# Sixteen-head attention on one core: the extra pieces of a step move into the bank of the burst of values

## The chip, the core and the metric

The kernel runs on one NeuronCore of a Trainium2 chip. Five engines run their own instruction queues: TensorE (PE in the profile; its weight loads are PEld), VectorE (DVE), ScalarE (ACT), GpSimd (POOL) and SyncE (SP, which here only starts transfers). The metric is device time of one execution in microseconds (us). Before the change the median of three runs is 1695.35 us (1690.04 to 1696.96). The profile comes from one further execution.

## What is computed

The input x is 8 sequences of 512 tokens with 128 features. Four layers follow each other, each with a residual and a layer norm. The change concerns the first and third, two attentions with 16 heads of 8 features:

```python
qkv = x @ W_qkv.T + b_qkv                        # 128 -> 3 * 128
scores = einsum('bhqd,bhkd->bhqk', q, k) / sqrt(8)
probs = softmax(scores + bias)                   # layer 0 only: bias = -slope[h] * |i - j|
out = einsum('bhqk,bhkd->bhqd', probs, v)
x = layernorm(x + out @ W_out.T + b_out)
```

The second layer is a gated feed-forward with operands rounded to a 4-bit grid in blocks of 16; the fourth is two blocks of windowed attention and a gated feed-forward. The change does not touch these two.

## The kernel before

Both attentions run through one function, `attention(li, ...)` (L250), with li 0 or 1. The work is cut into units: one sequence b and one group g of four heads, 32 units in all. `q` and `k` of a sequence lie transposed in SBUF as eight pairs of heads, one head in partitions 0 to 63 and one in 64 to 127, in two buffers that sequences take in turn. A unit is 8 half-steps of scores and, 16 half-steps later (`LAG`), 8 half-steps of weights. The main loop (L467) takes two half-steps at a time; this text calls one turn of it a step, and places are counted in half-steps, so a unit is 4 steps and a sequence 16 steps (places 0, 2, ... 30).

In each step PE gets, for t = 0 and 1:

- `scores`: two matmuls of 512 columns into a tile `s_ps` of two PSUM banks (pool `as`, two such tiles). DVE reduces it to the row maxima `m`.
- `weights`: the transposed product of another unit, two matmuls into two banks `t_ps`, in layer 0 with small corrections for the bias (`corrected`). ACT takes the exponential of each into `e` (four per step, 512 columns each).

Then come the extras, which a dictionary `todo`, filled by `later(place, function, ...)` in `plan` (L403), holds for each place:

- `values` (L338), one in each step: a burst of 16 matmuls that multiply a unit's exponentials with the values of its heads, into 128 columns of a bank `av`. The values carry a column of ones, so the sums of the softmax come out beside the products. ACT copies `av` into `avs`.
- `shift` (L324), one step in four: one transposition of `m` into `m_ps`, an ACT copy `mt`, two small DMAs started by POOL, which put the negative maxima into the last row of `q`.
- a piece, in 12 of 16 steps: `divide` (a unit's four transposes into `o_ps`, a reciprocal and a multiply on DVE), `begin_x`, `begin_qk` and `begin_v` (transpose and projections of the next sequence: `xt_ps`, `qk_ps`, `v_ps`, each taken out by ACT), `end_o` and `end_y` (transpose and output projection of the finished sequence: `ot_ps`, taken out by ACT, and `y_ps`, added to `xs` by DVE). `measured` takes the statistics of the result.

`begin_qk` further splits its result into two parts on POOL (a cast and a subtraction), SP writes them to DRAM (`far`), and `load_qk` reads them back in the layout of `q` or `k` with eight DMAs per quarter.

The PSUM tiles of pool `at` have two names, t0 and t1, with two banks each. Step z calls `weights` with rings z % 2 and then (z + 1) % 2, so each call takes both banks of one name. The extras of step z take banks of name z % 2: the burst one, the piece the other, a shift likewise. In the next step that name is used by the second `weights`.

PE runs in program order, `Kept` and `tc.keep_in_program_order` hold the written order on all engines, and the tile framework adds the waits. The loop also chooses the order inside a step: where the step before held a piece (`pieces`, L466), `weights` stands ahead of `scores`, otherwise behind:

```python
for f, a in sorted(todo.pop(z), key=lambda x: first.index(x[0]) if x[0] in first else len(first)):
    f(*a)        # first = [values, shift]; then the pieces
```

In the profile all matmuls of the attentions have line L256 and all transposes L257 (the helpers `mm` and `tr`), what goes through `Kept` has L48, SP's writes of `far` L225 and its reads L237. So instructions are told apart by their tiles.

Of the kernel before, what the change touches and what calls it, by code (L numbers as in the profile page):

```python
# [9 lines left out]
F32 = mybir.dt.float32  # L10
# [4 lines left out]
ALU = mybir.AluOpType  # L15
# [3 lines left out]
P = 128  # L19
B, S, D = 8, 512, 128  # L20
# [31 lines left out]
def body(ctx, tc, x, consts, rows, wa0, wa1, acols, bo, wf, wqkv, wo, w1, w2, cols, b2r, qs, ks, out):  # L52
# [136 lines left out]
    def in_tiles(mm, dst, lhsT, rhs):  # L189

        for r in range(0, P, 32):
            mm(dst[r : r + 32], lhsT=lhsT[:, r : r + 32], rhs=rhs, start=True, stop=True)

    def operand_steps(li, qs_, ks_, va, mm, tr, bank, work, dram, qb):
        w, col = wa[li], acol[:, li]

        def begin_x(b, h):
            ps = bank("xt_ps")
            for c in range(NT):
                tr(ps[:, c * P : (c + 1) * P], xn[:, b * NT + c, :], ident)  # L200
            h["xT"] = work.tile([P, S], F32, tag="xT", name="xT", bufs=1)
            act_.copy(h["xT"], ps)

        def begin_qk(b, h, n, start=nc.sync.dma_start, part=None):

            at = slice(0, S) if part is None else slice(part * S // 2, (part + 1) * S // 2)
            ps = bank("qk_ps")[:, at]
            in_tiles(mm, ps, w[:, n * P : (n + 1) * P], h["xT"][:, at])
            if part != 1:
                h["x"] = work.tile([P, S], F32, tag="x", name="x", bufs=1)  # L210
            t = h["x"]
            if n == 0:
                act_.activation(t[:, at], ps, AF.Identity, bias=qb, scale=col[:, 0:1])
            else:
                act_.activation(t[:, at], ps, AF.Identity, bias=col[:, 2:3])
            if part == 0:
                return
            parts = work.tile([P, 2, S], F32R, tag=f"hl{n}", name="parts", bufs=1)
            hi, lo = parts[:, 0, :], parts[:, 1, :]
            pool_.tensor_copy(hi, t)  # L220
            pool_.tensor_tensor(lo, t, hi.bitcast(F32), ALU.subtract)

            far = dram.tile([2, 2, 64, S], F32R, tag=f"far{n}", name="far")
            for j in range(2):
                start(  # L225
                    out=far[j].bitcast(F32).rearrange("a c t -> c a t"), in_=parts[64 * j : 64 * j + 64].bitcast(F32)
                )
            h["far", n] = far

        def load_qk(b, h, n, part, start=nc.sync.dma_start):  # L230

# [9 lines left out]
        def begin_v(b, h):  # L241
            ps = bank("v_ps").rearrange("p (c d) -> p c d", c=NT)
            for c in range(NT):
                in_tiles(mm, ps[:, c, :], h["xT"][:, c * P : (c + 1) * P], w[:, W_V : W_V + P])
            act_.copy(va[b % 2][:, :, :, 0:8], ps.rearrange("p c (h d) -> p c h d", d=8))

        return begin_x, begin_qk, load_qk, begin_v


    def attention(li, alibi, qs_, ks_, va, batch, late=None, spare=None, alone=0):  # L250
# [7 lines left out]
        with ExitStack() as st:  # L258
# [3 lines left out]
            def bank(name, n=None):  # L262
# [2 lines left out]
                    n = turn[0]  # L265
                return p_t.tile([P, S], F32, tag=f"t{n}", name=name)

            begun = len(batch)
            batch += [{} for _ in range(B - begun)]
            work = crow = None  # L270

            def hold_o(h):
                h["o"] = work.tile([P, NT, P], F32, tag="o", name="o", bufs=3)

            def with_bias(b):
                for c in range(NT):
# [46 lines left out]

            def shift(u):  # L324

                ps = bank("m_ps")[0:16, 0:P]
                tr(ps, u["m"].rearrange("p j a c -> p (j a c)"), ident)
                mt = small.tile([16, P], F32R, tag="mt", name="mt")
                act_.copy(mt, ps)
# [8 lines left out]
            def values(u, pp, c):  # L338

                if pp == 0 and c == 0:  # L340
                    u["avs"] = work.tile([P, NT, P], F32, tag="avs", name="avs")
                av = bank("av")[:, 0:P]
                for blk in range(NT):
                    for j in range(2):
                        for f in range(2):
# [6 lines left out]
                act_.copy(u["avs"][:, 2 * pp + c, :], av)  # L352

            def divide(u):

                ps = bank("o_ps")
                to = ps.rearrange("p (f c a j d) -> p f c a j d", f=2, c=2, a=2, j=2)
                for i in range(NT):
                    tr(to[:, :, i % 2, i // 2], u["avs"][:, i, :], ident)
                ps = ps.rearrange("p (n r c) -> p n r c", n=NT, r=4)  # L360
                den = work.tile([P, NT, 4], F32, tag="den", name="den")
                dve.reciprocal(den, ps[:, :, :, 8])
                g = u["g"]
                dve.tensor_tensor(
                    u["h"]["o"][:, :, g * 32 : (g + 1) * 32].rearrange("p c (r d) -> p c r d", d=8),
                    ps[:, :, :, 0:8],
                    den.unsqueeze(3).broadcast_to([P, NT, 4, 8]),
                    ALU.mult,
                )
                u["e"] = u["avs"] = None  # L370

            def end_o(h):
                ps = bank("ot_ps")
                for c in range(NT):
                    tr(ps[:, c * P : (c + 1) * P], h["o"][:, c, :], ident)
                h["oT"] = work.tile([P, S], F32, tag="oT", name="oT", bufs=1)
                act_.copy(h["oT"], ps)

            def end_y(b, h):
                ps = bank("y_ps").rearrange("p (c d) -> p c d", c=NT)  # L380
                for c in range(NT):
                    in_tiles(mm, ps[:, c, :], h["oT"][:, c * P : (c + 1) * P], w[:, W_O : W_O + P])
                i0, h["bn"] = b * NT, small.tile([P, NT, 6], F32, tag="bn", name="bn")
                dve.tensor_tensor(xs[:, i0 : i0 + NT, :], ps, xs[:, i0 : i0 + NT, :], ALU.add)

            def measured(b, h, lo, hi):
                for c in range(lo, hi):
# [15 lines left out]
            def plan():  # L403
# [1 line left out]
                const, work = pool("ac", 1), pool("aw", 2)  # L405
                dram = pool("ad", 2, space=bass.MemoryType.DRAM)
                begin_x, begin_qk, load_qk, begin_v = operand_steps(
                    li, qs_, ks_, va, mm, tr, bank, work, dram, qb[:, li : li + 1]
                )

                bvb = const.tile([P, P], F32, name="bvb")
# [3 lines left out]
                for n in range(B * G):  # L415
# [3 lines left out]
                    for i in range(NT):  # L419
                        later(z + 4 + 2 * i, values, units[n], *divmod(i, 2))  # L420
                    if g == 0 and begun <= b + 1 < B:
                        nxt = (b + 1, batch[b + 1])
                        order = (0, 6, 8, 14, 16) if b else (8, 10, 12, 14, 16)
                        for at, f in zip(order, (begin_x, *[begin_qk] * 4)):
                            i = order.index(at) - 1
                            later(s + at, f, *nxt, *((i // 2, nc.sync.dma_start, i % 2) if i >= 0 else ()))
                        for at, n_, part in ((14, 0, 0), (18, 0, 1), (22, 1, 0), (26, 1, 1)):
                            later(s + at, load_qk, *nxt, n_, part)
                        later(s + 22, begin_v, *nxt)
                        later(s + 22, with_bias, b + 1)  # L430
                    if g == 0:
                        later(s + 20 if b else alone, hold_o, batch[b])
                    if g == G - 1:
                        if b < B - 1:
                            times = (z + 16, z + 22, z + 24, z + 26)
                        else:
                            times = (z + 14, z + 16, z + 16, z + 16)
                        later(times[0], end_o, batch[b])
                        later(times[1], end_y, b, batch[b])
                        later(times[2], measured, b, batch[b], 0, 2)  # L440
                        later(times[3], measured, b, batch[b], 2, NT)
# [17 lines left out]
                if late:  # L459
                    late()  # L460
                if spare:
                    spare(later, lambda b: (b * G + G - 1) * NU + LAG + 32, work, bank, mm, tr, p_s)
                turn[1] = 0

            first, loaded = [values, shift], False
# [1 line left out]
            for z in range((B * G * NU + LAG + 20) // 2):  # L467
# [1 line left out]
                    plan()  # L469
                n, i = divmod(2 * z, NU)  # L470
                m, k = divmod(2 * z - LAG, NU)
                turn[0] = z % 2
                heavy, loaded = loaded, any(f.__name__ in pieces for f, _ in todo.get(z, []))
                for t in range(2):
                    if 0 <= m < B * G and heavy:
# [699 lines left out]
    with tc.tile_pool(name="ops", bufs=1) as ops:  # L1175
# [27 lines left out]
        def first_spare(later, done, work, bank, mm, tr, p_s):  # L1203
# [3 lines left out]
                quantize_weights(later, 28 + 11 * j, j, temps, work, bank, tr)  # L1207

            def tokens(b):
                for i, f in zip((0, 4, 6, 8), quantized_tokens(b, *temps(), work)):  # L1210
                    later(done(b) + i, f)

            for b in range(B - 1):
# [14 lines left out]
            h, end = {}, done(B - 1) - 32 + 4 * NT  # L1228
# [66 lines left out]
def _attention_layout(w_qkv, b_qkv, w_out):  # L1295
# [6 lines left out]
    w[:, W_O : W_O + P] = w_out.T  # L1302
    c = np.zeros((P, 4), np.float32)
    c[:, 1], c[:, 2], c[:, 3] = b_qkv[0:P][order], b_qkv[P : 2 * P][order], b_qkv[2 * P :]
    return w, c, order // 8


# [40 lines left out]
```

## Time and profile before

| | |
|---|---|
| profiled execution, its own time | 1685.9 us |
| its span, first to last instruction | 1684.1 us |
| granted TensorE clock, mean | 0.969 |
| busy: PE, DVE, ACT, POOL | 1563.3, 1372.5, 1264.0, 915.5 us |
| bursts of values of layer 0, first to last of 126 | 63.9 to 464.8 us |
| bursts of values of layer 1, first to last of 126 | 604.8 to 976.3 us |
| two more bursts per layer follow another without a pause and are counted with it | |

Between the two lie the rest of layer 0 and the feed-forward; after 980 us the fourth layer runs, 42% of the span. A line of the timeline gives start, duration, engine, source line, operation, output tile, input tiles, shapes, and in brackets how long the engine was idle before it and what ended that. The duration of a merged line (x4) covers all of its instructions. A burst's line shows x32, since each fp32 matmul is issued as two.

### The profile page before, as it was taken

To read this page: it belongs to the slowest core of one execution; us is meant where nothing else is said; L and a number is where in the kernel's file an instruction comes from. 1 tells how busy PE (TensorE), PEld (TensorE's weight loads), DVE (VectorE), ACT (ScalarE), POOL (GpSimd) and SP (SyncE) were. 2 spreads that over 40 slices of the span, in tenths; PEclk is the share of its full clock that TensorE was granted. 3 is DMA by queue.
4 is the path that set the end of the run, shared out by engine and by line. 5 is a ranking of instruction groups with operands and counts; after the bars stand their busy time and mean duration, and the time that the engine had idled before them with its cause. 6 is when DMAs were issued, how large, how long until landed. Compare 5 with 4: busy or idle time off the path is not lost.

```text
span 1684.1 us, 50766 instructions
## 1 busy us (share of the span) xinstructions
PE 1563.3 (93%) x20544; PEld 1056.3 (63%) x20545; DVE 1372.5 (81%) x2220; ACT 1264.0 (75%) x3214; POOL 915.5 (54%) x974
## 2 busy tenths in 40 slices
PE   2989999999988899999999879999999999999995
PEld 1556766666655656666666556666666666666664
DVE  3878888898578998888889668888888888888863
ACT  0577888888745578888888767788888888888873
POOL 3222323332247722333322469888888888888882
PEclk7899999999998889999999999999999999999998
DMA  6733233222010432332222121111111111111110
GB/s 123 150 76 98 53 78 78 59 49 57 11 13 1 76 78 78 78 78 62 60 61 69 30 53 33 39 36 36 37 38 36 36 36 36 42 42 42 36 36 25
DMA packets 92843, 90.79 MB, mean 54 GB/s; under 512 B 45969, under 2 KB 58257, under 8 KB 92610
## 3 DMA queue, kind: packets, MB, share of 16 engines
q1 hardware_dynamic: 87280, 85.49, 23.0%
q8 instruction: 163, 2.67, 0.7%
q10 hardware_dynamic: 1234, 1.52, 0.4%
q0 software_dynamic: 4096, 0.54, 0.2%
q14 instruction: 70, 0.57, 0.1%
HBM read 41.82 MB, written 18.87 MB: 36 GB/s over the span
## 4 chain that ended last, share of the span: by engine, by line
PE 70%; DVE 14%; ACT 5%; POOL 5%; DMA 3%; issue 2%; SPq 0%; ACTq 0%; DVEq 0%; POOLq 0%
PE av L256 13%; PE t_ps L256 10%; PE s_ps L256 7%; DVE m L48 6%; PE y_ps L671 6%; PE sp L671 5%; PE o_ps L671 3%; PE t_ps L671 3%; PE v_ps L671 3%; PE q_ps L671 3%; PE k_ps L671 3%; PE p_ps L671 3%; PE gp L671 2%; ACT e L48 2%; PE ap L671 2%
## 5 line engine op out<-in xcount | busy, mean ns | idle before, releaser
L48 DVE TENSOR_REDUCE m<-s_ps 128x2 f32<-128x1024 f32 x512 | 600.0, 1219 | 90.6 <-PE s_ps L256 84.7
L48 ACT ACTIVATE e<-t_ps 128x512 f32<-128x512 f32 x1024 | 530.2, 603 | 103.0 <-PE t_ps L256 101.9
L256 PE MATMUL s_ps<-k,q 63*128 63x512 f32 x1024 | 281.2, 477 | 40.3 <-DVE m L48 19.4
L256 PE MATMUL av<-e,va 128*32 128x128 f32 x8192 | 279.4, 278 | 14.2 <-ACT e L48 9.0
L256 PE MATMUL t_ps<-q,k 64*128 64x512 f32 x1024 | 270.3, 450 | 2.5 <-DMA q<-mt 0.9
L256 PEld LDWEIGHTS av<-e,va 128*32 128x32 f32 x8192 | 210.9, 110 | 87.3 <-ACT e L48 73.0
L48 POOL DMA_DIRECT2D q<-mt x128 | 68.9, 542 | 348.0 <-ACT mt L48 347.8
L671 ACT ACTIVATE pw<-sp,m,was_v 128x128 f32<-128x128 f32 x512 | 227.5, 479 | 1.6 <-DVE m L671 0.9
L671 POOL TENSOR_TENSOR was_v<-was_v 128x16 f32<-128x16 f32 x64 | 187.8, 2934 | 5.3
L256 PEld LDWEIGHTS t_ps<-q,k 64*128 64x128 f32 x1024 | 133.4, 187 | 85.1 <-ACT avs L48 34.0
L256 PEld LDWEIGHTS s_ps<-k,q 63*128 63x128 f32 x1024 | 120.9, 192 | 76.7 <-DVE m L48 41.6
L671 POOL TENSOR_TENSOR pw<-pw,den 128x1024 f32<-128x1024 f32 x64 | 121.3, 1895 | 7.6 <-DVE den L671 7.6
L671 ACT ACTIVATION_READ_ACCUMULATOR pw<-sp,m,was_v 128x1 f32 x512 | 115.2, 225 | 0.0
L48 POOL CAST parts<-x 128x512 fp32r<-128x512 f32 x32 | 21.7, 678 | 163.9 <-ACT x L48 163.9
L671 DVE TENSOR_REDUCE m<-sp 128x4 f32<-128x512 f32 x128 | 82.3, 684 | 19.0 <-PE sp L671 17.2
L671 ACT COPY v<-v_ps 128x512 f32<-128x512 f32 x64 | 37.7, 590 | 71.6 <-PE v_ps L671 71.6
L671 POOL TENSOR_TENSOR was_k<-was_k,was_q 128x512 f32<-128x512 f32 x64 | 88.1, 1377 | 0.9 <-DVE was_q L671 0.9
L671 PEld LDWEIGHTS t_ps<-cst,was_k 128*128 128x128 f32 x512 | 59.2, 142 | 44.4 <-issue 22.1
L671 DVE COPY pT<-p_ps 128x512 f32<-128x512 f32 x128 | 79.9, 665 | 0.5 <-PE p_ps L671 0.5
L671 PEld LDWEIGHTS p_ps<-cst,pw 128*128 128x128 f32 x512 | 59.8, 141 | 32.3 <-issue 28.0
L48 ACT COPY avs<-av 128x128 f32<-128x128 f32 x256 | 71.1, 278 | 11.6 <-PE av L256 8.7
L671 DVE TENSOR_REDUCE was_v<-was_k 128x16 f32<-128x1024 f32 x64 | 77.1, 1205 | 0.0
(191 smaller groups left out, 3252.8 us busy)
## 6 DMA issues: line engine op xcount, KB each, us to landing
far<-parts SPq DMA_DIRECT2D x64, 256.0 KB
q<-far SPq DMA_DIRECT2D x256, 64.0 KB
k<-far SPq DMA_DIRECT2D x240, 64.0 KB
ve<-v SPq DMA_DIRECT2D x112, 128.0 KB
xn<-in_x SPq DMA_DIRECT2D x8, 256.0 KB
q<-mt POOLq DMA_DIRECT2D x128, 4.0 KB, 3.2
hn<-xs SPq DMA_DIRECT2D x16, 128.0 KB
hn<-xs SPq DMA_DIRECT2D x16, 112.0 KB
```

Source lines behind the costliest of these rows:

```text
L48: return lambda *a, **k: self.tc.keep_in_program_order(f(*a, **k))
L256: mm = lambda *a, **k: tc.keep_in_program_order(nc.tensor.matmul(*a, **k))
L671: kept = lambda f: lambda *a, **k: tc.keep_in_program_order(f(*a, **k))
```

## The change

- A new helper `share(name, lo, n)` gives columns of one bank per step. The burst of values takes columns 0 to 128, a shift columns 128 to 256, a piece columns 256 to 512. If columns are taken already, a new bank is begun; at each step the bank is forgotten.
- All pieces are cut to 256 columns: transposes, values, the output transposes and the output projection of a sequence come as two halves (`part` 0 and 1) at two places; q's and k's projections were halves already. They take one bank's columns 256 to 512 each.
- `divide` writes its four transposes at 9-column distances, each over the unused tail of the one before, in four blocks of 60 columns (240 in all), and multiplies in two halves. The order of features in `o` changes; the rows of the output weights and of the value bias are permuted alike on the host.
- Places within a sequence's 16 steps change: `begin_x` from 0 to 6 and 8; q from 6, 8 to 10, 14; k from 14, 16 to 16, 18; `begin_v` from 22 to 26 and 30; `load_qk` from 14, 18, 22, 26 to 16, 18, 22, 24; `end_o` from 24 to 22 and 24; `end_y` from 30 to 0 and 2 of the next sequence; statistics and the quantization of layer 0's tokens follow. Now each of the 16 steps holds a piece, and the four with a shift hold both.

```diff
+            shared = {"at": None}
+            def share(name, lo=S // 2, n=S // 2):
+                if shared["at"] is None or any(lo < b and a < lo + n for a, b in shared["used"]):
+                    shared["at"], shared["used"] = bank(name), []
+                shared["used"].append((lo, lo + n))
+                return shared["at"][:, lo : lo + n]
...
+        def piece(name, part):
+            if part is None:
+                return bank(name), slice(0, S), range(NT)
+            ps = share(name) if share else bank(name)[:, 0 : S // 2]
+            return ps, slice(part * S // 2, (part + 1) * S // 2), range(2 * part, 2 * part + 2)
...
-        def begin_x(b, h):
-            ps = bank("xt_ps")
-            for c in range(NT):
-                tr(ps[:, c * P : (c + 1) * P], xn[:, b * NT + c, :], ident)
-            h["xT"] = work.tile([P, S], F32, tag="xT", name="xT", bufs=1)
-            act_.copy(h["xT"], ps)
+        def begin_x(b, h, part=None):
+            ps, at, chunks = piece("xt_ps", part)
+            for i, c in enumerate(chunks):
+                tr(ps[:, i * P : (i + 1) * P], xn[:, b * NT + c, :], ident)
+            if part != 1:
+                h["xT"] = work.tile([P, S], F32, tag="xT", name="xT", bufs=1)
+            act_.copy(h["xT"][:, at], ps)
...
-                ps = bank("m_ps")[0:16, 0:P]
+                ps = share("m_ps", P, P)[0:16]
...
-                av = bank("av")[:, 0:P]
+                av = share("av", 0, P)
...
-                ps = bank("o_ps")
-                to = ps.rearrange("p (f c a j d) -> p f c a j d", f=2, c=2, a=2, j=2)
+                ps = share("o_ps")[:, 0:240].rearrange("p (r k) -> p r k", r=4)
                 for i in range(NT):
-                    tr(to[:, :, i % 2, i // 2], u["avs"][:, i, :], ident)
+                    tr(ps[:, :, 9 * i : 9 * i + 32], u["avs"][:, i, :], ident)
+                ps = ps[:, :, 0:36].rearrange("p r (i d) -> p r i d", d=9)
...
+                for f in range(2):
+                    both = slice(2 * f, 2 * f + 2)
+                    dve.tensor_tensor(
+                        u["h"]["o"][:, 4 * f : 4 * f + 4, at : at + 16].rearrange("p i (j d) -> p i j d", d=8),
+                        ps[:, both, :, 0:8].rearrange("p j i d -> p i j d"),
+                        den[:, both, :].rearrange("p j i -> p i j").unsqueeze(3).broadcast_to([P, NT, 2, 8]),
+                        ALU.mult,
+                    )
...
+                        for part in range(2):
+                            later(s + (6 if b else 8) + 2 * part, begin_x, *nxt, part)
+                            later(s + (10, 14)[part], begin_qk, *nxt, 0, sp, part)
+                            later(s + (16, 18)[part], begin_qk, *nxt, 1, sp, part)
+                            later(s + (26, 30)[part], begin_v, *nxt, part)
...
+                        times = (14, 16, 24, 26, 26, 30) if b < B - 1 else (14, 14, 16, 16, 16, 16)
+                        for i, f in enumerate((end_o, end_o, end_y, end_y, measured, measured)):
...
-                turn[0] = z % 2
+                turn[0], shared["at"] = z % 2, None
```

More of the change, by code (lines that the diff above doesn't have):

```diff
@@ L192, in in_tiles, with operand_steps @@
             mm(dst[r : r + 32], lhsT=lhsT[:, r : r + 32], rhs=rhs, start=True, stop=True)
-    def operand_steps(li, qs_, ks_, va, mm, tr, bank, work, dram, qb):
+    def operand_steps(li, qs_, ks_, va, mm, tr, bank, work, dram, qb, share=None):
         w, col = wa[li], acol[:, li]
-        def begin_x(b, h):
-            ps = bank("xt_ps")
-            for c in range(NT):
-                tr(ps[:, c * P : (c + 1) * P], xn[:, b * NT + c, :], ident)
-            h["xT"] = work.tile([P, S], F32, tag="xT", name="xT", bufs=1)
-            act_.copy(h["xT"], ps)
+        def piece(name, part):
[10 more added lines that the diff above has]
+            act_.copy(h["xT"][:, at], ps)
         def begin_qk(b, h, n, start=nc.sync.dma_start, part=None):
-            at = slice(0, S) if part is None else slice(part * S // 2, (part + 1) * S // 2)
-            ps = bank("qk_ps")[:, at]
+            ps, at, _ = piece("qk_ps", part)
             in_tiles(mm, ps, w[:, n * P : (n + 1) * P], h["xT"][:, at])
@@ L239, in load_qk, with begin_v @@
                     )
[L241 to L245, printed above, removed]
+        def begin_v(b, h, part=None):
+            ps, _, chunks = piece("v_ps", part)
+            ps = ps.rearrange("p (c d) -> p c d", d=P)
+            for i, c in enumerate(chunks):
+                in_tiles(mm, ps[:, i, :], h["xT"][:, c * P : (c + 1) * P], w[:, W_V : W_V + P])
+            act_.copy(va[b % 2][:, chunks[0] : chunks[-1] + 1, :, 0:8], ps.rearrange("p c (h d) -> p c h d", d=8))
         return begin_x, begin_qk, load_qk, begin_v
@@ L272, in hold_o @@
             def hold_o(h):
-                h["o"] = work.tile([P, NT, P], F32, tag="o", name="o", bufs=3)
+                h["o"] = work.tile([P, 2 * NT, 64], F32, tag="o", name="o", bufs=3)
             def with_bias(b):
@@ L351, in values @@
                             )
-                act_.copy(u["avs"][:, 2 * pp + c, :], av)
+                act_.copy(u["avs"][:, 2 * c + pp, :], av)
             def divide(u):
-                ps = bank("o_ps")
-                to = ps.rearrange("p (f c a j d) -> p f c a j d", f=2, c=2, a=2, j=2)
+                ps = share("o_ps")[:, 0:240].rearrange("p (r k) -> p r k", r=4)
                 for i in range(NT):
-                    tr(to[:, :, i % 2, i // 2], u["avs"][:, i, :], ident)
-                ps = ps.rearrange("p (n r c) -> p n r c", n=NT, r=4)
@@ L361, in divide @@
-                den = work.tile([P, NT, 4], F32, tag="den", name="den")
+                    tr(ps[:, :, 9 * i : 9 * i + 32], u["avs"][:, i, :], ident)
+                ps = ps[:, :, 0:36].rearrange("p r (i d) -> p r i d", d=9)
+                den = work.tile([P, 4, NT], F32, tag="den", name="den")
                 dve.reciprocal(den, ps[:, :, :, 8])
[L363 to L369, printed above, removed]
@@ L370, in divide @@
-                u["e"] = u["avs"] = None
[L372 to L384, printed above, removed]
+                at = 16 * u["g"]
@@ new lines, in end_o, with end_y @@
+            def end_o(h, part):
+                ps = share("ot_ps")
+                for n in range(2):
+                    at = 4 * part + 2 * n
+                    tr(ps[:, n * P : (n + 1) * P], h["o"][:, at : at + 2, :].rearrange("p a d -> p (a d)"), ident)
+                if part == 0:
+                    h["oT"] = work.tile([P, S], F32, tag="oT", name="oT", bufs=1)
+                act_.copy(h["oT"][:, part * S // 2 : (part + 1) * S // 2], ps)
+            def end_y(b, h, part):
+                ps = share("y_ps").rearrange("p (c d) -> p c d", c=2)
+                for n in range(2):
+                    at = (2 * part + n) * P
+                    in_tiles(mm, ps[:, n, :], h["oT"][:, at : at + P], w[:, W_O : W_O + P])
+                i0 = b * NT + 2 * part
+                if part == 0:
+                    h["bn"] = small.tile([P, NT, 6], F32, tag="bn", name="bn")
+                dve.tensor_tensor(xs[:, i0 : i0 + 2, :], ps, xs[:, i0 : i0 + 2, :], ALU.add)
@@ L407, in plan @@
                 begin_x, begin_qk, load_qk, begin_v = operand_steps(
-                    li, qs_, ks_, va, mm, tr, bank, work, dram, qb[:, li : li + 1]
+                    li, qs_, ks_, va, mm, tr, bank, work, dram, qb[:, li : li + 1], share
                 )
@@ L421, in plan @@
                     if g == 0 and begun <= b + 1 < B:
[L422 to L427, printed above, removed]
+                        nxt, sp = (b + 1, batch[b + 1]), nc.sync.dma_start
+                        for part in range(2):
[3 more added lines that the diff above has]
+                            later(s + (26, 30)[part], begin_v, *nxt, part)
+                        for at, n_, part in ((16, 0, 0), (18, 0, 1), (22, 1, 0), (24, 1, 1)):
                             later(s + at, load_qk, *nxt, n_, part)
-                        later(s + 22, begin_v, *nxt)
                         later(s + 22, with_bias, b + 1)
@@ L433, in plan @@
                     if g == G - 1:
[L434 to L441, printed above, removed]
+                        times = (14, 16, 24, 26, 26, 30) if b < B - 1 else (14, 14, 16, 16, 16, 16)
+                        for i, f in enumerate((end_o, end_o, end_y, end_y, measured, measured)):
+                            of = (i % 2,) if i < 4 else (2 * (i % 2), 2 * (i % 2) + 2)
+                            later(z + times[i], f, *(() if i < 2 else (b,)), batch[b], *of)
                 if not begun:
@@ L461, in plan @@
                 if spare:
-                    spare(later, lambda b: (b * G + G - 1) * NU + LAG + 32, work, bank, mm, tr, p_s)
+                    spare(later, lambda b: (b * G + G - 1) * NU + LAG + 38, work, bank, mm, tr, p_s)
                 turn[1] = 0
@@ L1209, in tokens @@
             def tokens(b):
-                for i, f in zip((0, 4, 6, 8), quantized_tokens(b, *temps(), work)):
+                for i, f in zip((0, 4, 8, 10), quantized_tokens(b, *temps(), work)):
                     later(done(b) + i, f)
@@ L1226, in table @@
                 act_.activation(one, half[:, 0:1], AF.Silu)
-            h, end = {}, done(B - 1) - 32 + 4 * NT
+            h, end = {}, done(B - 1) - 22
             later(end - 1, turned)
@@ L1301, in _attention_layout @@
     w[:, W_V : W_V + P] = w_qkv[2 * P :].T
[L1302 removed]
+    by = np.arange(P).reshape(4, 2, 16).transpose(1, 0, 2).reshape(-1)
+    w[:, W_O : W_O + P] = w_out.T[by]
     c = np.zeros((P, 4), np.float32)
[L1304 removed]
+    c[:, 1], c[:, 2], c[:, 3] = b_qkv[0:P][order], b_qkv[P : 2 * P][order], b_qkv[2 * P :][by]
     return w, c, order // 8
```

## The prediction

> **What bounds the kernel now.** I read the page first (busy shares, the 40 slices), then windows of busy time to find the stages, then the timeline of one attention stage, instruction by instruction. The page:
>
> ```profile
> span 1684.1 us, 50766 instructions
> PE 1563.3 (93%) x20544; PEld 1056.3 (63%) x20545; DVE 1372.5 (81%) x2220; ACT 1264.0 (75%) x3214; POOL 915.5 (54%) x974
> PE 70%; DVE 14%; ACT 5%; POOL 5%; DMA 3%; issue 2%; SPq 0%; ACTq 0%; DVEq 0%; POOLq 0%
> L48 ACT COPY avs<-av 128x128 f32<-128x128 f32 x256 | 71.1, 278 | 11.6 <-PE av L256 8.7
> ```
>
> PE is busy nearly always and carries 70% of the chain that ended last. The change touches only the two attentions; their bursts of values run from 63.9 to 464.8 us (layer 0) and from 604.8 to 976.3 us (layer 1). There busy time by windows is, in the steady part of each:
>
> ```profile
> 240.00:420.00 180.00, 174.21 (x3161) 122.44 (x3160) 160.65 (x206) 145.94 (x324) 57.63 (x83) 1.00 0.27 58
> 660.00:900.00 240.00, 237.44 (x3870) 154.01 (x3869) 209.50 (x250) 202.50 (x464) 72.17 (x112) 1.00 0.29 70
> ```
>
> (Columns: window, length, busy PE, PEld, DVE, ACT, POOL, granted clock, DMA share, GB/s.) No engine is idle long; the clock is full. So what matters is how the engines hand work to each other inside a step. Two consecutive kinds of step from the timeline of layer 1, first one with a projection piece (qk_ps), then one with the transposes of a unit (o_ps):
>
> ```profile
> 641.09 0.81 PEld L256 LDWEIGHTS av<-e,va 128*32 128x32 f32 x32 [0.36 <-ACT e L48]
> 641.88 0.24 PEld L256 LDWEIGHTS qk_ps<-xT,wa 128*32 128x32 f32 x8
> 642.24 0.27 ACT L48 COPY avs<-av 128x128 f32<-128x128 f32 x1
> 642.54 0.19 PEld L256 LDWEIGHTS t_ps<-q,k 64*128 64x128 f32 x2 [0.41 <-ACT avs L48]
> 642.76 0.47 ACT L48 ACTIVATE x<-qk_ps,acol 128x256 f32<-128x256 f32 x1 [0.25 <-PE qk_ps L256]
> ...
> 647.74 0.28 PE L257 MATMUL m_ps<-cst,m 128*16 128x128 f32 x1
> 647.87 0.27 ACT L48 COPY avs<-av 128x128 f32<-128x128 f32 x1
> 647.94 0.19 PEld L256 LDWEIGHTS s_ps<-k,q 63*128 63x128 f32 x2
> 648.05 0.26 ACT L48 CAST mt<-m_ps 16x128 fp32r<-16x128 f32 x1
> ...
> 649.36 0.81 PEld L256 LDWEIGHTS av<-e,va 128*32 128x32 f32 x32 [0.48 <-ACT e L48]
> 650.37 0.42 PEld L257 LDWEIGHTS o_ps<-cst,avs 128*128 128x128 f32 x4 [0.20 <-ACT e L48]
> 650.64 0.30 ACT L48 COPY avs<-av 128x128 f32<-128x128 f32 x1
> 650.96 0.19 PEld L256 LDWEIGHTS t_ps<-q,k 64*128 64x128 f32 x2 [0.17 <-ACT avs L48]
> 651.36 0.29 DVE L48 TENSOR_TENSOR o<-o_ps,den 128x128 f32<-128x128 f32 x1
> 651.77 0.18 PEld L256 LDWEIGHTS t_ps<-q,k 64*128 64x128 f32 x1 [0.28 <-PE s_ps L256]
> ```
>
> The reader is to see that PE starts the piece 0.79 us (qk) or 1.01 us (transposes) after the burst av began, while ACT starts the copy of av only 1.15 us after it (641.09 to 642.24; 1.28 in the last case) and needs 0.27 more. The piece stands in the other bank, so it runs while ACT waits for and copies av: it is free cover.
>
> A step's length, from the first weight load of one burst to that of the next (means over all steps of a kind; layer 1 / layer 0): qk 2.86 / 2.99; xt 2.99 / 3.17; v 3.32 / 3.48; ot 3.01 / 3.16; y 3.47 / 3.54; o 3.15 / 3.28; m_ps alone 2.71 / 3.06. One step of 10.17 (layer 0) and one of 4.47 are left out. It splits into a (first t_ps load to burst) + d (burst to piece) + p (piece to the next t_ps load): qk is 1.41 + 0.79 + 0.66 = 2.86, o at its median 1.47 + 1.01 + 0.58 = 3.06.
>
> **The change part by part.**
>
> *Sharing the bank of the burst.* In the built program of the changed kernel every piece's first matmul waits for the ACT instruction that copies the same step's av; before it waits for the second exponential of the step, done long ago. That the columns differ does not matter: the wait is on the tile. So d becomes 1.15 (burst to copy) + 0.27 (copy) + 0.05 (a copy's end to a waiting load: the x copy ends at 643.23, its waiter loads at 643.28) = 1.47. That is +0.68 for projections, +0.46 for transposes. Behind the piece PE's queue holds the next step's t_ps, so ACT's exponentials and DVE's maxima are late by the same amount; nothing covers it, since ACT has finished the four exponentials by then.
>
> The row shows a piece's matmuls and ACT's copy at one time in two banks. The Trainium skill ("PSUM — Partial Sum Buffer", PSUM bank collisions raise a hardware error) says engines must be kept apart by bank and 32-partition quadrant, not by address, and both sides here span all partitions: by it the overlap is lost whatever the columns, the sum below; by a reading by address the wait would be nothing and the sum about -8. No run here shows such a collision.
>
> *The shift steps.* m_ps moves to columns 128 to 256 of the same bank, ahead of the piece. It waits for av's copy and the piece waits for the cast of mt: m_ps to cast 0.31, cast 0.26, hand-over 0.05: +0.62 between copy and piece. Every shift step of an inner batch now also has a piece (second y half, one qk half of each kind, first v half); before none had.
>
> *Halves.* Two pieces of half the size stand in two steps. p: qk 0.66 as before; v and y 1.09 (653.22 to 654.31 in the timeline) become 0.55 each; four transposes 0.58, one 0.21, so two 0.33. The ACT copies of halves end before the exponentials could start (x: 0.47 within the 0.59 that the exponentials take to start anyway), so the added copies cost nothing; if the exponentials started earlier they would cost 0.1. The y half's add on DVE is about 0.42 between 0.29 (128 columns) and 0.69 (512): a is 1.50 there, not 1.62.
>
> *Divide.* The transposes still stream 128 columns each, now in runs of 32: p stays 0.58. Before, o_ps in runs of 64 and ot_ps unbroken both take 0.66, so I take nothing; the upper end is twice 0.58, +36 over 62. The same page (Specifications) says non-contiguous patterns slow matmuls significantly; it gives no figure. One multiply becomes two of 64 elements. Reciprocal (16 elements) takes 0.26 and the multiply (128) 0.29, so each is nearly all fixed cost: +0.3 on the chain reciprocal, multiply, t_ps (the load at 651.77), and a is 1.77. Ends: 0.05 to 0.3.
>
> *Steps after the change, layer 1:* o 1.77+1.47+0.58 = 3.82; xt and ot halves 1.41+1.47+0.33 = 3.21; qk 3.54; v half 3.43; y half 3.52; with shift +0.62. A batch of 16 steps: o 4 x 3.82 = 15.3; four transposed halves 12.8; qk 2 x 3.54 + 2 x 4.16 = 15.4; v 3.43 + 4.05; y 3.52 + 4.14: 58.7. Before: 4 x 3.15 + 2.99 + 4 x 2.86 + 3.32 + 3.01 + 3.47 + 4 x 2.71 = 47.7. So +11.0. Layer 0, whose a is 0.14 longer (the corrections; 0.16 for o): 61.0 against 50.7, +10.3.
>
> *Moved steps.* qk of q goes from steps 6, 8 to 10, 14 and of k from 14, 16 to 16, 18; with them POOL's cast and subtraction (0.61 + 1.28), SP's two writes (1.23) and 32 reads (from 14, 18, 22, 26 to 16, 18, 22, 24). SP's order of DMAs is unchanged. The reads are needed at step 32: the last have four steps (14 us) against 3.9 us of issuing eight. x has one buffer, and k's first half now comes one step after q's second: POOL needs 1.9 of the 3.5 us. Hidden; without that slack, up to 2 us a batch. Statistics, quantized tokens and values move by one to four steps off the path. One load of a weight behind the moved writes on SP holds DVE for 6.78 us at 122.6; its writes come a step later: +4 (0 to 8), once.
>
> *Sum:* 7 batches x 10.3 + 6 x 11.0 = 138; steps outside full batches (10 o at 0.7, 8 m_ps at 0.4, halves at the ends) 12; the load 4: +154. The profiled execution took 1685.9 (span 1684.1), giving 1840; it lies 9.5 below the median 1695.35, on which it gives 1849. I take 1845.
>
> **The rivals.**
> 1. *Partly hidden.* a holds a pause of PE for the exponential (0.36 before av). With DVE and ACT less pressed a could fall to 0.59 + 0.60 + 0.05 = 1.24, saving 0.17 in some 210 steps, and the second multiply may cost 0.05: together -50, 1795. For it: DVE waits shape layer 0. Against: a hardly differs between qk and xt.
> 2. *Dearer.* Short runs slow the transposes (+36), or POOL's slack fails (2 x 13): 1880 to 1905.
> 3. *Faster.* The piece's wait has already ended when PE gets there. Then a set of 16 steps costs 58.7 less 11.6 of waits (8 x 0.68 + 8 x 0.46 + 4 x 0.62) = 47.1 against 47.7, and t_ps, which waits 34.0 us in all for av's copy, finds the other bank free: 1655 to 1685. It decides only if the copy ended within about 0.05 us of where PE reaches the piece, against the 0.46 to 0.68 measured above.
> 4. *No change:* the wait's loss and the halves' gain cancel; nothing in the rows has that size.
>
> **How the numbers follow.** Forecast 0.68 (own range 1815 to 1870), partly hidden 0.17, dearer 0.09, faster 0.04, no change 0.02. The range 1785 to 1895 reaches from rival 1 to the lower end of rival 2. Within 0.5% (about 8 us) counts as no change, which is what measurements of this kernel can tell. Faster 0.04, same 0.02, slower 0.94.
>
> **What would show it.** In the changed profile: the piece's weight load starts 1.45 to 1.5 us after its burst, put down to ACT avs; PE waits for avs total some 100 us in place of 34.0; in shift steps the piece waits for ACT mt; ACT waits for t_ps more than 101.9; PE busy below 90%; the stages outside the attentions unchanged; qk steps 3.5, shift steps 4.1, o 3.8. I am wrong if pieces start within 1.1 us of the burst, or if a falls as d grows.

## The result

The changed kernel takes 1841.55 us (median of four runs, 1838.51 to 1846.60) where the kernel before took 1695.24 beside it: a ratio of 1.0872, with a 95% interval of 1.0838 to 1.0906. It is slower by 146 us, and the forecast of 1845 (1785 to 1895) holds. The profiled execution took 1841.17 us by its own time, 1839.2 by its span, at a mean granted clock of 0.964 (before 0.969). One execution of own_banks (below) took 3955.52 us where its other three took 1721.33 to 1722.09; its ratio leaves that one out, and as it is the profiled one, no length is read from that kernel's trace.

**The page after the change.** These lines answer to the four shown of before: the span, the busy times (share, number of instructions), the chain that ended last, and the row of the copy of `av`.

```profile
span 1839.2 us, 51149 instructions
PE 1600.8 (87%) x20545; PEld 1050.9 (57%) x20545; DVE 1376.0 (75%) x2300; ACT 1274.4 (69%) x3256; POOL 912.9 (50%) x974
PE 44%; ACT 12%; DVE 6%; POOL 4%; issue 3%; DMA 1%; SPq 0%; ACTq 0%; DVEq 0%; POOLq 0%
L48 ACT COPY avs<-av 128x128 f32<-128x128 f32 x256 | 72.4, 283 | 17.5 <-PE av L264 14.6
```

The work has hardly grown: DVE is busy 3.5 us longer, ACT 10.4, POOL 2.6 less, for a span that is 155 us longer. (PE shows 37.5 more for the same number of matmuls but one; where that comes from was not followed up.) The time lies in the gaps. PE falls from 93% to 87% busy and from 70% to 44% of the chain; ACT rises from 5% to 12%.

**Two windows in the steady parts of the attentions,** layer 0 and layer 1, columns as before (window, length, busy PE, PEld, DVE, ACT, POOL, clock, DMA share, GB/s):

```profile
240.00:420.00 180.00, 155.50 (x2687) 99.59 (x2680) 134.75 (x184) 125.59 (x287) 48.72 (x72) 1.00 0.24 55
800.00:1040.00 240.00, 203.46 (x3165) 126.59 (x3165) 173.03 (x225) 169.87 (x391) 57.51 (x90) 1.00 0.27 60
```

PE is busy 155.5 of 180 us where it was 174.2, and 203.5 of 240 where it was 237.4. DVE and ACT have lost about as much: every engine now waits, and the clock is still full. So it is the hand-over inside a step.

**Three steps from the timeline of layer 1:** a burst with a shift and half of the values, a burst with the four transposes of a unit, and a burst with half of the values. All tiles of a step's bank now go by the name `av`; the shift reads `cst,m`, the transposes `cst,avs`, the values `wa,xT`.

```profile
801.78 0.81 PEld L264 LDWEIGHTS av<-e,va 128*32 128x32 f32 x32 [0.41 <-ACT e L48]
...
803.06 0.30 ACT L48 COPY avs<-av 128x128 f32<-128x128 f32 x1
803.41 0.09 PEld L265 LDWEIGHTS av<-cst,m 128*16 128x16 f32 x1 [0.81 <-ACT avs L48]
...
803.73 0.25 ACT L48 CAST mt<-av 16x128 fp32r<-16x128 f32 x1 [0.37 <-PE av L265]
804.03 0.38 PEld L264 LDWEIGHTS av<-wa,xT 128*32 128x32 f32 x16 [0.54 <-ACT mt L48]
...
804.61 0.19 PEld L264 LDWEIGHTS t_ps<-q,k 64*128 64x128 f32 x2 [0.20 <-issue]
...
805.85 0.81 PEld L264 LDWEIGHTS av<-e,va 128*32 128x32 f32 x32 [0.39 <-ACT e L48]
...
807.12 0.30 ACT L48 COPY avs<-av 128x128 f32<-128x128 f32 x1
807.48 0.42 PEld L265 LDWEIGHTS av<-cst,avs 128*128 128x128 f32 x4 [0.81 <-ACT avs L48]
807.48 0.66 PE L265 MATMUL av<-cst,avs 128*128 128x128 f32 x4 [0.54 <-ACT avs L48]
...
808.24 0.26 DVE L48 RECIPROCAL den<-av 128x16 f32<-128x16 f32 x1 [0.49 <-PE av L265]
...
808.53 0.36 DVE L48 TENSOR_TENSOR o<-av,den 128x64 f32<-128x64 f32 x2
...
809.67 0.81 PEld L264 LDWEIGHTS av<-e,va 128*32 128x32 f32 x32 [0.37 <-ACT e L48]
...
810.82 0.27 ACT L48 COPY avs<-av 128x128 f32<-128x128 f32 x1
811.13 0.38 PEld L264 LDWEIGHTS av<-wa,xT 128*32 128x32 f32 x16 [0.65 <-ACT avs L48]
811.13 0.65 PE L264 MATMUL av<-wa,xT 128*32 128x128 f32 x16 [0.38 <-ACT avs L48]
```

Take the last burst: it begins at 809.67, the copy at 810.82 (1.15 later) ends at 811.09, and the piece starts at 811.13, which is 1.46 after the burst, released by `avs`. Before, a piece started 0.79 or 1.01 after it, and beside the copy, not behind it. In the first step the chain has two more links: copy, shift (803.41), cast of `mt` (803.73), piece (804.03): 2.25 after the burst.

**The waits of the whole run** (who waits, for whom: us in all, times, longest):

```profile
ACT e L48 <- PE t_ps L264: 136.3, 160, 3.1
...
PE av L265 <- ACT avs L48: 78.0, 174, 0.5
...
PE av L264 <- ACT avs L48: 21.2, 51, 0.5
...
PE av L264 <- ACT mt L48: 17.5, 51, 0.3
```

PE's matmuls wait 78.0 + 21.2 = 99.2 us for the copy and 17.5 for the cast, in rows that were not there before. One engine further on, ACT's exponentials wait 136.3 for `t_ps`, 34.4 more than before: they stand behind the late piece.

**By stages,** from the first and last burst of each attention: the time before layer 0 grew by 0.4 us, the bursts of layer 0 by 64.7 (400.9 to 465.6), the stretch between the attentions by 10.0 (140.0 to 150.0), the bursts of layer 1 by 78.8 (371.5 to 450.3), the rest by 1.2. That is 155.1, the whole growth of the span.

### The profile page after: what moved, and what is told of

Its sections match the earlier page's. It is cut to its first block, busy times and chain, and to the rows that moved or that the text cites. A ratio compares the mean times of both kernels' runs of the same rounds, so it can differ in the third digit from the quotient of the medians.

```text
span 1839.2 us, 51149 instructions
## 1 busy us (share of the span) xinstructions
PE 1600.8 (87%) x20545; PEld 1050.9 (57%) x20545; DVE 1376.0 (75%) x2300; ACT 1274.4 (69%) x3256; POOL 912.9 (50%) x974
## 4 chain that ended last, share of the span: by engine, by line
PE 44%; ACT 12%; DVE 6%; POOL 4%; issue 3%; DMA 1%; SPq 0%; ACTq 0%; DVEq 0%; POOLq 0%
ACT e L48 8%; PE y_ps L690 5%; PE t_ps L264 5%; PE sp L690 4%; PE av L264 4%; PE o_ps L690 3%; PE v_ps L690 3%; PE t_ps L690 3%; PE p_ps L690 2%; PE q_ps L690 2%; PE k_ps L690 2%; PE gp L690 2%; PE av L265 2%; PE ap L690 2%; PE s_ps L264 2%
## 5 line engine op out<-in xcount | busy, mean ns | idle before, releaser
L48 ACT ACTIVATE e<-t_ps 128x512 f32<-128x512 f32 x1024 | 529.1, 603 | 142.9 <-PE t_ps L264 136.3
L264 PE MATMUL s_ps<-k,q 63*128 63x512 f32 x1024 | 273.3, 466 | 34.5 <-DVE m L48 16.3
L264 PE MATMUL t_ps<-q,k 64*128 64x512 f32 x1024 | 276.9, 463 | 2.0 <-DMA q<-mt 0.9
L48 ACT COPY avs<-av 128x128 f32<-128x128 f32 x256 | 72.4, 283 | 17.5 <-PE av L264 14.6
L690 PE MATMUL y_ps<-wo_s,oT 128*128 128x128 f32 x512 | 74.8, 290 | 0.0
```

Of the source, the lines that this page charges most:

```text
L48: return lambda *a, **k: self.tc.keep_in_program_order(f(*a, **k))
L264: mm = lambda *a, **k: tc.keep_in_program_order(nc.tensor.matmul(*a, **k))
L690: kept = lambda f: lambda *a, **k: tc.keep_in_program_order(f(*a, **k))
```

## The experiments

The theory: the loss is the wait for the copy of the burst, which a piece in the same bank must sit out, and in shift steps the wait for the cast too; halves, moved places and the 9-column transposes cost next to nothing. The rivals: the halves and the moved places themselves cost, so that separate banks bring back only a part; the order on POOL's queue costs, by the moved quantization; the dense transposes or the second multiply cost. Ratios are to the kernel before, run beside each. Kernels that were run together shared one chip.

| kernel | median us | ratio, 95% interval |
|---|---|---|
| own_banks | 1721.86 | 1.0179 (1.0153 to 1.0205) |
| piece_apart | 1728.5 | 1.0235 (1.0204 to 1.0266) |
| shift_apart | 1804.63 | 1.0668 (1.0642 to 1.0694) |
| xqt_own | 1840.3 | 1.0874 (1.0851 to 1.0897) |
| early_tokens | 1834.62 | 1.0839 (1.0809 to 1.0869) |
| before_qk_shared | 1710.45 | 1.0106 (1.0073 to 1.0140) |
| apart_shift8 | 1691.6 | 1.0006 (0.9986 to 1.0025) |
| after_again | 1843.41 | 1.0893 (1.0865 to 1.0920) |
| early_again | 1833.61 | 1.0830 (1.0806 to 1.0855) |

The first four ran beside a kernel before of 1691.66, the next three beside 1690.71, the last two beside 1690.86.

**1. own_banks: no two tiles share a bank.** The changed kernel, but every request takes the next bank. The halves, places and dense transposes stay.

```diff
-                if shared["at"] is None or any(lo < b and a < lo + n for a, b in shared["used"]):
+                if True or any(lo < b and a < lo + n for a, b in shared["used"]):
```

> The changed kernel with the sharing alone taken back: each burst, shift and piece takes a whole bank again; halves, places and the 9-column transposes stay. Hand-over theory (the loss is the wait of a piece for the copy of av, and of a piece behind a shift for the cast of mt): pieces of steps without a shift start 0.79 or 1.01 us after their burst in place of 1.47 to 1.6; in steps with a shift the piece is the third taker of two banks, so it still waits for av's copy but no longer for mt: 1.47 in place of 2.1 to 2.2. Per full set of 16 steps 4 x 0.48 + 4 x 0.4 + 3 x 0.68 + 0.75 + 4 x 0.65 = 8.9 less, over 13 sets 116: about 1725 (1710 to 1745). Rival (the loss is the new schedule: a piece in every step, halves, weights always ahead of scores): stays at 1820 to 1845.

Measured 1721.86. Of some 150 us, 120 go when the bank is no longer shared. What is left is 30 us, and it has a candidate in the code: the name has two banks, so in the four shift steps of a sequence the third tile is the first bank again, and the piece waits for the copy there after all. The trace has this wait: 51 weight loads of `qk_ps`, `v_ps` and `y_ps` wait for `avs`, as many as there are shift steps with a piece. Together with the 8 to 10 us of experiment 5 that has the size; experiment 6, where no third tile is left, shows that, taken together, nothing else stays.

**2. shift_apart: the shift alone gets its own bank.**

```diff
-                ps = share("m_ps", P, P)[0:16]
+                ps = bank("m_ps")[0:16, 0:P]
```

> The changed kernel with m_ps alone in a bank of its own; av and the pieces still share. Hand-over theory: the second link goes, pieces in 50 shift steps start 0.62 us earlier (1.47 in place of 2.1), 9 shift steps without a piece gain 0.5: 35 us less, about 1806 (1798 to 1815). A rival in which one wait for ACT per step is all there is to lose, and mt's cast is hidden in it: 1835 to 1845.

Measured 1804.63 against 1806 expected. The shift step of layer 0 with a qk half falls from 4.32 to 3.70 us, with d (burst to piece) from 2.10 to 1.48: just the 0.62 that the prediction gave to the link of shift and cast. In all it is worth 0.020 to 0.022 of 1691 us (1.0872 and 1.0893 less 1.0668), 35 to 38 us.

**3. before_qk_shared: the kernel before, with one kind of piece sharing.** Nothing is halved or moved here; q's and k's projections, which were halves already, go to columns 256 to 512 of the burst's bank, and all else stays.

```diff
-            ps = bank("qk_ps")[:, at]
+            ps = share("qk_ps") if share and part is not None else bank("qk_ps")[:, at]
...
-                av = bank("av")[:, 0:P]
+                av = share("av", 0, P)
```

> The kernel before with one dose of the change: the halves of q's and k's projections (49 steps) go to columns 256 to 512 of the burst's bank, all else as before. Hand-over theory: 0.68 us for each of them, +33: about 1725 (1718 to 1730). Rival (the schedule and not the shared bank): no change, 1688 to 1696.

Measured 1710.45: slower by 19.7 us (12 to 24 by the interval), where 33 were expected. The mechanism is there without any other part of the change. The timeline of one such step and the waits of the run:

```profile
700.99 0.27 ACT L48 COPY avs<-av 128x128 f32<-128x128 f32 x1
701.30 0.16 PEld L256 LDWEIGHTS av<-xT,wa 128*32 128x32 f32 x8 [0.65 <-ACT avs L48]
...
701.87 0.19 PEld L256 LDWEIGHTS t_ps<-q,k 64*128 64x128 f32 x2 [0.41 <-issue]
```

```profile
PEld av L256 <- ACT avs L48: 31.4, 48, 0.7
...
PE av L256 <- ACT avs L48: 18.5, 48, 0.4
```

The piece loads 0.04 after the copy's end (701.26 to 701.30), and from there to `t_ps` it is 0.57. The size was off for two reasons that the steps show. d rose by 0.68 as said (0.79 to 1.47), but p (piece to the next `t_ps` load) fell from 0.65 to 0.57, so a qk step of layer 1 rose from 2.86 to 3.44 and one of layer 0 from 2.99 to 3.59: 0.59 on each of 48, 28 us. And in layer 0 the 29 steps with `m_ps` alone fell from 3.06 to 2.81 on average, 7 us. That DVE catches up in the longer steps would give this; it was not tried by itself.

**4. piece_apart: the pieces get banks of their own, the shift stays with the burst and goes behind the piece.**

```diff
+                if lo == S // 2:
+                    return bank(name)[:, lo : lo + n]
...
-            first, loaded = [values, shift], False
+            first, loaded = {values: 0, shift: 2}, False
```

> The changed kernel with pieces in a bank of their own and queued ahead of the shift, which alone shares the burst's bank. Hand-over theory: no piece waits for av or mt; a shift's transposition finds av's copy done (1.42) when the piece ends (0.79 + 0.57), and t_ps follows at about 1.7 where it is 2.7 now. Per set 5.7 to 6.3 from the twelve other steps and 4 x 1.0: about 10, over 13 sets 130: about 1710 (1690 to 1725), near the kernel before. Schedule rival: 1820 to 1845.

Measured 1728.5, 18 above the number: a miss, and a useful one. d is 1.01 and 0.79 again, so the banks do what the theory says. But a wait of another kind has appeared, here in the waits and in the timeline:

```profile
PE t_ps L264 <- DMA q<-mt: 21.2, 18, 2.6
```

```profile
780.24 0.24 ACT L48 CAST mt<-av 16x128 fp32r<-16x128 f32 x1
...
780.40 0.61 POOL L48 CAST parts<-x 128x512 fp32r<-128x512 f32 x1 [3.64 <-ACT x L48]
...
781.09 1.28 POOL L48 TENSOR_TENSOR parts<-x,parts 128x512 fp32r<-128x512 f32 x1
...
782.32 1.05 POOL L48 DMA_DIRECT2D q<-mt  x2
...
788.46 0.51 PEld L264 LDWEIGHTS t_ps<-q,k 64*128 64x128 f32 x2 [2.82 <-issue]
788.49 0.98 PE L264 MATMUL t_ps<-q,k 64*128 64x512 f32 x2 [2.61 <-DMA q<-mt]
```

`mt` is ready at 780.48. POOL, which starts the DMAs, works in order, and since the shift is now written behind the piece, the piece's cast and subtraction (0.61 and 1.28) come first; the DMAs start at 782.32, and at 788.49 PE's first use of the unit has stood 2.61 us for them. Putting the shift last was mine, not the change's.

**5. xqt_own and early_tokens: the 10 us between the attentions.** In the changed kernel the feed-forward's first matmul waits once, for long. PE's wait, then the timeline of POOL and ACT there:

```profile
PE gu L48 <- ACT xqT L48: 8.0, 1, 8.0
```

```profile
538.12 0.57 POOL L48 TENSOR_SCALAR rstd<-stats 128x4 f32<-128x4 f32 x1 [6.26 <-DVE stats L48]
...
539.92 3.12 POOL L48 TENSOR_SCALAR xn<-xs,stats,rstd 128x128 f32<-128x128 f32 x4
...
543.01 1.05 POOL L48 TENSOR_TENSOR xs<-qy,sc 128x512 f32<-128x512 f32 x1
...
544.09 0.37 ACT L48 COPY xqT<-xq_ps 128x256 f32<-128x256 f32 x1 [8.91 <-POOL xs L48]
```

`xs<-qy` is the last write of the quantization of the seventh sequence. The change moved its steps later, so on POOL it now stands behind the layer norm of the eighth, which waits for its statistics. In the kernel before it stood ahead of that layer norm:

```profile
466.16 1.06 POOL L48 TENSOR_TENSOR xs<-qy,sc 128x512 f32<-128x512 f32 x1 [7.84 <-DVE qy L48]
...
475.09 3.16 POOL L48 TENSOR_SCALAR xn<-xs,stats,rstd 128x128 f32<-128x128 f32 x4
```

In the changed kernel ACT's `xqT` takes the buffer of `qy`, so it waits for that write. Two edits tell whether it is the buffer or the place in the queue. xqt_own gives `xqT` another buffer:

```diff
-                ps, h["xT"] = bank("xq_ps")[:, 0 : 2 * P], work.tile([P, S], F32, tag="qy", name="xqT", bufs=1)
+                ps, h["xT"] = bank("xq_ps")[:, 0 : 2 * P], work.tile([P, S], F32, tag="xT", name="xqT", bufs=1)
```

> The changed kernel with xqT, the operand of the first gate of the feed-forward at the end of layer 0, in another buffer than the quantized tokens. If the 10 us by which the stretch between the last burst of layer 0 and the first of layer 1 grew (140 to 150) come from ACT's wait of 8.9 us for POOL's last write out of that buffer: about 1833 (1830 to 1836). If POOL or DVE are late there anyway: 1841.

Measured 1840.3, no gain: a miss. The stretch is 146.9 us instead of 150.0. The wait has moved on; in its timeline ACT's next instruction of the feed-forward now waits for the same write on POOL:

```profile
550.28 1.05 POOL L48 TENSOR_TENSOR xs<-qy,sc 128x512 f32<-128x512 f32 x1
551.37 0.82 ACT L519 ACTIVATE si<-gu 128x352 f32<-128x352 f32 x2 [6.71 <-POOL xs L48]
```

early_tokens leaves the buffer and issues the seventh sequence's quantization four to six places earlier:

```diff
-                for i, f in zip((0, 4, 8, 10), quantized_tokens(b, *temps(), work)):
+                last = b == B - 2
+                for i, f in zip((-4, 0, 2, 4) if last else (0, 4, 8, 10), quantized_tokens(b, *temps(), work)):
...
-                later(done(b), tokens, b)
+                later(done(b) - (4 if b == B - 2 else 0), tokens, b)
```

> The changed kernel with the quantization of the seventh sequence's tokens four to six half-steps earlier, so that POOL's last write of it stands ahead of the last sequence's layer norm (four normalizations, 3.1 us) on POOL's queue again and not behind it. If the 10 us between the two attentions come from this order: 8 to 10 less than the changed kernel, about 1832. If they come from elsewhere (DVE, the clock, the first units of layer 1): 1838 to 1843.

Measured 1834.62; the stretch is 141.8 us. The ratio's interval overlapped that of the changed kernel, so both were run once more, side by side:

> The changed kernel once more, on the same chip and against the same runs as the next one, so that 6 to 10 us can be told. 1838 to 1843.

> The changed kernel with the seventh sequence's tokens quantized earlier, again. If POOL's order between the two attentions costs 8 to 10 us: 8 to 10 less than the changed kernel beside it. If the 6 of the first comparison were the difference of two chips: the same within 3.

1843.41 and 1833.61: 9.8 us less, with intervals that no longer meet (1.0865 to 1.0920, 1.0806 to 1.0855). On POOL the write now stands ahead of the layer norm:

```profile
536.17 1.06 POOL L48 TENSOR_TENSOR xs<-qy,sc 128x512 f32<-128x512 f32 x1 [8.44 <-DVE qy L48]
...
542.08 3.12 POOL L48 TENSOR_SCALAR xn<-xs,stats,rstd 128x128 f32<-128x128 f32 x4
```

So the rival of POOL's order holds for some 8 to 10 us of the 150, and the place in the queue is the cause; the buffer only carried it to the next engine.

**6. apart_shift8: all three together.** Separate banks for pieces as in piece_apart, the quantization as in early_tokens, and the shift one step earlier, so that its DMAs come ahead of the cast of `x` on POOL:

```diff
-                later(n * NU + 10, shift, units[n])
+                later(n * NU + 8, shift, units[n])
```

> Halves and places of the change without its waits: pieces in a bank of their own, the shift behind the piece in the burst's bank and one step earlier (place 8 of a unit in place of 10), so that its DMAs no longer stand behind a cast and a subtraction on POOL; the seventh sequence's tokens early. Hand-over theory: the 21 us that PE waited for the shift's DMA where pieces stood apart go, and the 8 to 10 us between the attentions: about 1700. By the medians of steps without such waits (46.7 and 50.0 a set against 47.7 and 50.7 before) it could reach 1683. Rival: the moved schedule costs of itself, so 1715 or more.

Measured 1691.6, a ratio of 1.0006 (0.9986 to 1.0025): the kernel before, to a quarter of a per cent. The wait for the DMAs is gone:

```profile
PE t_ps L264 <- DMA q<-mt: 0.2, 1, 0.2
```

This kernel still has every half, every moved piece, the dense transposes and the second multiply. So the rivals of the halves, the places and the transposes fall as causes of a loss: together those cost no more than 4 us (the interval's upper end, 0.0025 of 1691), net of a gain that hides in them: halved pieces shorten a (see rival 1 below), by an estimate some 12 us in all (0.12 to 0.21 in six of 16 steps, over 13 sets), and other parts of the moved schedule cost about as much here. Against the loss of 150 us both are small. From piece_apart it is 37 us less; 21 are the wait that went and 8 to 10 the quantization, the remaining 6 to 8 are not told apart. None of these kernels beats the one before.

## Why the prediction was right

Steps by kind, median us (T is the step, d burst to piece, p piece to the next `t_ps` load, a from there to the next burst; layer 1 up to 1050 us, with T predicted, and layer 0):

| step | layer 1: T predicted | T | d | p | a | layer 0: T | d | p | a |
|---|---|---|---|---|---|---|---|---|---|
| o (four transposes) | 3.82 | 3.68 | 1.49 | .59 | 1.60 | 3.81 | 1.47 | .59 | 1.75 |
| xt half | 3.21 | 3.16 | 1.55 | .37 | 1.24 | 3.31 | 1.49 | .37 | 1.44 |
| ot half | 3.21 | 3.16 | 1.55 | .37 | 1.24 | 3.31 | 1.48 | .37 | 1.44 |
| qk | 3.54 | 3.45 | 1.47 | .57 | 1.41 | 3.61 | 1.46 | .57 | 1.57 |
| v half | 3.43 | 3.29 | 1.47 | .57 | 1.25 | 3.48 | 1.47 | .57 | 1.44 |
| y half | 3.52 | 3.57 | 1.62 | .57 | 1.38 | 3.58 | 1.50 | .57 | 1.50 |
| shift + qk | 4.16 | 4.11 | 2.17 | .57 | 1.37 | 4.32 | 2.10 | .57 | 1.64 |
| shift + v half | 4.05 | 4.07 | 2.25 | .57 | 1.24 | 4.16 | 2.12 | .57 | 1.45 |
| shift + y half | 4.14 | 4.06 | 2.12 | .57 | 1.38 | 4.17 | 2.09 | .57 | 1.51 |

- *Sharing the bank.* Right: d was predicted at 1.47, and most kinds stand at 1.46 to 1.50; the release is by `avs`. Where d is longer, the copy starts later: in the steps at 801.78 and 805.85 above 1.28 and 1.27 after the burst, since ACT is then still at the four exponentials (2.07 us from 801.13), and d is 1.63. The wait is the whole of it: with banks apart the loss is gone, with one kind of piece sharing it is there.
- *The shift's chain, +0.62.* Right: d goes from 1.48 at `m_ps` to 2.10, and giving the shift its own bank brings 0.62 a step.
- *Halves.* p 0.57 for v and y against 0.55, and 0.37 for two transposes against 0.33. For qk 0.66 was taken over from before and 0.57 was measured. Before, the piece's weights were loaded ahead of its first matmul: the load at 641.88 starts 0.11 ahead of the matmul at 641.99. After, load and matmul start together (811.13), so the tenth that p held belongs to d. The prediction moved d and left p: the same 0.1 was counted twice.
- *The divide.* Right on the transposes: 0.66 for four in runs of 32 elements, as before in runs of 64 (`o_ps`) or unbroken (`ot_ps`); the +36 of rival 2, and its lack of slack on POOL, did not occur. The Trainium skill ("PSUM — Partial Sum Buffer", Specifications) says that non-contiguous patterns slow matmuls significantly; for this form no run here shows it. Mis-sized was the second multiply: two of 64 elements take 0.36 together, one of 128 took 0.29, and a of the o step rose by 0.12 to 0.13, not by 0.3. This is inside the ends of 0.05 to 0.3, but the upper end was taken because each instruction looked nearly all fixed cost. Two that stand back to back do not pay it twice in full.
- *Rival 1, a falls as d grows.* a does fall, but not because d grows. For the halves of xt, ot and v it goes from 1.40 to 1.44 down to 1.24 in layer 1, the very number of the rival, and from 1.56 to 1.59 down to 1.44 in layer 0; in qk it does not fall, and in o it rises. In apart_shift8, where d is back at 0.79 and 1.01, the same halves have an a of 1.19 to 1.25 and of 1.44 to 1.45. So it is the halving. The last `t_ps` load of a step stands behind ACT's copy of the piece, and the copy of a half is shorter (a step with values, before and after):

```profile
654.45 0.59 ACT L48 COPY va<-v_ps 128x512 f32<-128x512 f32 x1 [0.61 <-PE v_ps L256]
...
655.08 0.18 PEld L256 LDWEIGHTS t_ps<-q,k 64*128 64x128 f32 x1 [0.25 <-ACT va L48]
...
811.85 0.38 ACT L48 COPY va<-av 128x256 f32<-128x256 f32 x1 [0.76 <-PE av L264]
...
812.04 0.41 PEld L264 LDWEIGHTS t_ps<-q,k 64*128 64x128 f32 x2
```

The part "Halves" of the prediction took the 1.41 of qk for them: 0.17 too long for each in layer 1. ACT's copy of a qk half takes 0.47 to 0.56, that of theirs 0.37 to 0.38. For xt and ot it is paid back in part by a longer d. A set of 16 steps came to 57.7 in layer 1 (means, 58.7 predicted) and 59.8 in layer 0 (61.0 predicted).

- *Rival 3, the wait already over.* Excluded by d.
- *The moved steps.* Reads, writes and the cast of `x` are hidden, as said: PE waits 0.9 us in all for the shift's DMAs before and after. The late load of a weight costs one step of 13.24 where before one of 10.17 and one of 4.47 stood; above the usual steps of their kinds (3.31; 3.48 and 3.16) that is 9.9 against 8.0, so 2 of the 4.
- *"Statistics, quantized tokens and values move by one to four steps off the path."* Wrong for one of the eight sequences, at 10 us. The prediction looked at the path inside the attention. The last sequences have none behind them to hide in: POOL's order there decides when the feed-forward starts.
- *The sum* is right to 1 us against the profiled span's growth (+154 and +155), and that is partly luck. By stages, with the 12 of the steps outside full sets split as 3 in layer 0 and 9 in layer 1, it reads: layer 0 72 + 3 + 4 = 79 predicted, 64.7 measured; layer 1 66 + 9 = 75 predicted, 78.8 measured; the stretch between 0 predicted, 10.0 measured. So layer 0 was predicted 14 too dear, and the 10 of the stretch and the 4 of layer 1 made up for it. Of the 14, the full sets are 8 (7 x 1.2) and the load 2; the other 4 were not followed up. In layer 1 the full sets were under the number (6 x 10.0 = 60), and the steps outside them cost 19 instead of 9: near its end stand steps of 5.0 to 6.2 beside the first pieces of the fourth layer (before 4.1 to 4.8). Why those grew by more was not followed up.
- *What would show it.* PE's waits for `avs` are 99.2 us (about 100 said). But the 34.0 put beside it was a row of weight loads, and by those rows it is 124.9 + 34.8 = 159.7: the two kinds must not be mixed. PE at 87%, ACT's wait, the shift's release by `mt`, the start of the pieces and the step lengths came as said, o 0.14 under; the stages outside did not stay unchanged.

That a piece could run beside the copy in one bank without the wait was not tried, since the order of the two would then be open.

## What to carry to other kernels

Here, where a wait is on the tile, columns of a PSUM bank were free only to a producer that need not wait for a reader in it. Before packing two results into one bank, find who reads the first, and add what the second would wait (here 1.15 us to the copy, 0.27 for it, 0.05 for the hand-over, less where the piece started before) once for each step. Count it per step, and work out the sum from where the next work on the same engine starts, since a piece that is late makes everything queued behind it late. A piece cut in half can gain of itself, where the next work waits for the copy that empties its bank: predict that apart from the wait. When a change moves work in a queue that runs in order, look also at the last round of the loop, where no further round covers a moved instruction, and at the instructions that a DMA start will stand behind.

## What the runs showed of the hardware that was not expected

- Two small multiplies on VectorE that follow each other directly take 0.36 us for both (64 elements each), one of twice the size took 0.29: splitting it added 0.07, not another 0.26 to 0.29.
- Going from a piece whose weights are loaded 32 columns at a time to `t_ps`, PE's weight queue pauses 0.20 us (804.61, in the row as "issue"); from a transpose, loaded 128 columns at a time, it is 0.17 (808.06 in the timeline). No instruction that the profile shows ends it.
- Where a wait for another engine stands ahead of a piece, its weight load loses its lead of 0.11 us over the matmul: at 811.13 both start at one time. The wait holds the load too.
